# Two chained causal attentions: turning the maxima and packing the values by transfers instead of on TensorE

## The chip, the cores and the metric

The kernel runs on one core of a Trainium2 chip. TensorE multiplies matrices, VectorE, ScalarE and GpSimd (POOL in the profile) do the rest, and SyncE (SP) issues transfers. The metric is the device time of one execution in microseconds, the median of several runs. Everything is float32; many operands of TensorE are marked float32r.

## The reference, cut to what matters

There are 32 sequences of 512 tokens and 256 channels. Each is one block: two chained attentions, a layer norm, experts, a second layer norm. The experts act on the first sequence only, since their tokens are 512.

```python
q, k = x @ W_attn + b_attn          # 16 heads of 16 channels
v = x                               # by heads
y  = causal_attn(q, k, v)
e  = v[1:] - y[:-1]
k2 = x[:-1] @ W_k2 + b_k2
y2 = causal_attn(q[1:], k2, e)      # a row of zeros is put ahead of it
x = layernorm(x + y @ W_proj + b_proj + y2 @ W_proj + b_proj)
x = layernorm(x + experts(x))
```

The second attention takes its values from the results of the first, one token on.

## The kernel before, in words

A *group* is four heads of one sequence; there are 4 groups a sequence and 128 in all. The program is a software pipeline of *steps*, one for each group (`step`, L654). A step has five *slots* and a *gap* after each (`rest[0]` to `rest[4]`). The order of TensorE's and SP's instructions is the program's own (L67); the queues of VectorE, ScalarE and GpSimd are ordered by a scheduler when the program is built. Every queue is worked off in its order.

A slot (L393) interleaves two streams of small products on quarters of TensorE's array:
- `maxima` (L271), tiles `sm`: queries by keys for both attentions (a = 0 and 1), with a bfloat16 product that hides what is not causal. VectorE takes the largest score of each query (L325, tile `top`). The tiles `sm` take two pairs of banks of PSUM in turn, one for each pair of heads. So a slot can only begin its first product once VectorE has read the pair of the slot before.
- `scores` (L353), tiles `sc`: the same products transposed, keys by queries, of a group one or two steps older. The negated maximum is added by a third product (`k == 2`, L363), whose moving operand is `m`. ScalarE takes the exponential (L382), GpSimd hides the diagonal block (L386).

In the gaps:
- `project` (L219, tiles `pj`) makes queries and keys of a pair of groups (`two`); ScalarE adds the bias (`pk`), GpSimd splits it into two float32r parts (`lead`, `pk`), and `spread` (L243) copies these by SP's transfers into the interleaved layout `q_t` and `kk_t`.
- `halve` and `augment` (L329, L334) split a group's maxima into two parts, turn them on TensorE (four transposes, tile `mt`) and copy them to `m` by ScalarE. `m` is used from slot 2 of the next step.
- `values` (L426, tiles `av`) multiplies the exponentials with the values, for the first attention in gap 1 and for the second in gap 4 (two steps after the maxima). The 17th column of each head is 1, so it gives the sum of the exponentials. ScalarE copies the result (`avs`).
- `normalize` (L444) turns `avs` back by four transposes (tile `yt`) and divides by the sums. For the first attention the result gives `e_pad`, the values of the second (GpSimd, L474); it stands in gap 2. For the second it is added to `y` (L478), in gap 3 of the next step.
- `turn` (L509, eight transposes a sequence, tile `ys`) turns `y` for the output projection, `attended` (L518, tiles `po`), which comes two to four steps later, with a layer norm on VectorE and GpSimd.

SP issues all transfers of the loop: eight a step for `spread`, plus each sequence's loads and its store.

Of the kernel before, what the change touches and what calls it, by code (L numbers as in the profile page):

```python
# [17 lines left out]
P = 128  # L18
# [3 lines left out]
NH2 = 2  # L22
EPS = 1e-5
PER = 4
HV = HD + 1
# [14 lines left out]
def block_kernel(  # L40
# [32 lines left out]
    psum = ctx.enter_context(tc.tile_pool(name="psum", bufs=1, space=bass.MemoryType.PSUM))  # L73

# [101 lines left out]

    v_pad = const.tile([P, NB, NG * GH * HV + HS - HV], F32, name="v_pad")
    e_pad = const.tile([P, NB, NG * GH * HV + HS - HV], F32, name="e_pad")
# [3 lines left out]
    mx = [const.tile([P, NB, GH, HS], F32, name=f"mx{i}") for i in range(2)]  # L182
    for t in mx:
        nc.vector.memset(t, 0.0)
# [3 lines left out]
    def by_head(t):  # L188
        return t[:, :, 0 : NG * GH * HV].rearrange("p n (h s) -> p n h s", s=HV)


    groups = {}
    moving = {}

# [15 lines left out]
    def prepare(n):  # L210
        b, g = divmod(n, NG)
        s = seqs[b]
        heads = slice(g * GH, (g + 1) * GH)
        nc.gpsimd.tensor_copy(
            by_head(v_pad)[:, :, heads, 0:HD], s["x"].rearrange("p n (h d) -> p n h d", d=HD)[:, :, heads]
        )
# [26 lines left out]
    def spread(two, m, which=range(2)):  # L243

        for k in which:
            n = 2 * two + k
            d = groups.setdefault(n, {})
            d["q"] = q_t[n % len(q_t)]
            d["kk"] = kk_t[n % len(kk_t)]
            rows = slice(k * GH * HD, (k + 1) * GH * HD)  # L250
            for i, t in enumerate(moving[two, m]):
                if m == 0:
                    for r in range(2):
                        nc.sync.dma_start(d["q"][r::2, i], t[rows])
                else:
                    nc.sync.dma_start(d["kk"][i::2, m - 1], t[rows])
        if 1 in which:
            del moving[two, m]

    units = [
        ([(2, 0, 1, 0), (0, 0, 1, 3)], 2, 1, (0, 2)),
        ([(3, 0, 1, 0)], 3, 1, (0, 1)),
        ([(1, 0, 2, 0)], 1, 2, (1, 3)),
        ([(2, 1, 1, 0), (0, 1, 1, 3)], 2, 1, (2, 4)),
        ([(3, 1, 1, 0)], 3, 1, (2, 3)),
    ]

    def maxima(n, u, pair):  # L271
# [44 lines left out]
        for i, a, na, at in parts:  # L316
            to = d["top"][:, i, NH2 * pair : NH2 * (pair + 1), a : a + na]
            if alone:
                views += [(part(ps[hh], i, na, at), to[:, hh : hh + 1]) for hh in range(NH2)]
            else:  # L320
                views.append((part(ps[0], i, na, at), to))
# [7 lines left out]
    def halve(n):  # L329
        t, top = mx[n % 2], groups[n]["top"]  # L330
        nc.vector.tensor_copy(half(t[:, :, :, 0:2]), top)
        nc.vector.tensor_sub(half(t[:, :, :, 2:4]), top, t[:, :, :, 0:2])

    def augment(n):  # L334
        d = groups[n]
        ps = bank(f"mt{n}")
        for i in range(NB):
            nc.tensor.transpose(ps[:, i * P : (i + 1) * P], mx[n % 2][:, i].rearrange("p h s -> p (h s)"), ident)  # L338
        d["m"] = grp.tile([P, T], F32, tag="m", name=f"m{n}")
        nc.scalar.copy(half(d["m"]), ps)  # L340

    banks = [
        [(1, 0, 0)],
        [(1, 1, 0), (1, 3, 3)],
        [(0, 2, 0), (1, 2, 2)],
        [(0, 0, 0)],
        [(0, 1, 0), (0, 3, 3)],  # L350
    ]

    def scores(n, u, pair):  # L353
        parts = [p for p in banks[u] if 0 <= n - p[0] < n_all]
# [7 lines left out]
        def score(d, a, j, at, k, hh, rows):  # L362
            keys = minus[a][rows] if k == 2 else d["kk"][rows, a, j * P : (j + 1) * P]  # L363
            queries = d["m"][rows] if k == 2 else d["q"][rows, k]
            nc.tensor.matmul(  # L365
                ps[hh][:, at * P : at * P + T - j * P],
                half(keys),
                half(queries[:, j * P :]),
                start=(k == 0),
                stop=(k == 2),  # L370
            )

        for a, j, at in parts:
            groups[n - a]["pt", a, j, pair] = pt[:, :, at * P : at * P + T - j * P]
            for k in range(3):
                todo.append((T - j * P, partial(score, groups[n - a], a, j, at, k)))

        def exponentials():
# [5 lines left out]
            for a, j, at in parts:  # L384
# [41 lines left out]
    def values(n, a):  # L426
# [3 lines left out]
        ps = bank(f"av{n}_{a}")  # L430
        order = [0, 2, 1, 3] if a == 0 else [0, 1, 3, 2]
        for j in order:
            for h in range(GH):
                nc.tensor.matmul(  # L434
                    ps[HS * h : HS * (h + 1), j * P :],
                    vals[:, j, (g * GH + h) * HV : (g * GH + h) * HV + HS],
                    d["pt", a, j, h // NH2][:, h % NH2],
# [3 lines left out]
        avs = d["avs", a] = work.tile([P, T], F32, tag="avs", name=f"avs{n}_{a}")  # L441
        nc.scalar.copy(avs, ps)  # L442

    def normalize(n, a):  # L444
        b, g = divmod(n, NG)
        d, s = groups[n], seqs[b]
        ps = bank(f"yt{n}_{a}")
        for i in range(NB):
            nc.tensor.transpose(ps[:, i * P : (i + 1) * P], d["avs", a][:, i * P : (i + 1) * P], ident)  # L449
        got = ps.rearrange("p (n h s) -> p n h s", h=GH, s=HS)  # L450
        if a:

            kept = work.tile([P, NB, GH, HV], F32, tag="kept", name=f"kept{n}", bufs=2)
            nc.scalar.copy(kept, got[:, :, :, 0:HV])
            got = kept
        rden = small.tile([P, NB, GH], F32, tag="rden", name=f"rden{n}_{a}")
        sums = got[:, :, :, HD]
        if a:

            den = small.tile([P, NB, GH], F32, tag="den", name=f"den{n}")  # L460
            nc.vector.tensor_scalar_max(den, sums, 1e-30)
            sums = den
        nc.vector.reciprocal(rden, sums)
        rb = rden.unsqueeze(3).to_broadcast([P, NB, GH, HD])
        cols = slice(g * GH * HD, (g + 1) * GH * HD)

        def heads(t):
            return t[:, :, cols].rearrange("p n (h d) -> p n h d", d=HD)

        if a == 0:  # L470
            if g == 0:
                s["y"] = seq.tile([P, NB, C], F32, tag="y", name=f"y{b}")
            nc.vector.tensor_mul(heads(s["y"]), got[:, :, :, 0:HD], rb)
            nc.gpsimd.tensor_sub(by_head(e_pad)[:, :, g * GH : (g + 1) * GH, 0:HD], heads(s["xs"]), heads(s["y"]))  # L474
        else:
            y2 = work.tile([P, NB, GH * HD], F32, tag="y2", name=f"y2_{n}", bufs=1)
            nc.vector.tensor_mul(y2.rearrange("p n (h d) -> p n h d", d=HD), got[:, :, :, 0:HD], rb)
            nc.gpsimd.tensor_add(s["y"][:, :, cols], s["y"][:, :, cols], y2)  # L478
            groups.pop(n)
# [28 lines left out]

    def turn(b):  # L509
        s = seqs[b]  # L510
        ysT = s["ysT"] = work.tile([P, NC, T], F32, tag="ysT", name=f"ysT{b}", bufs=1)
        for c in range(NC):
            ps = bank(f"ys{b}_{c}")
            for i in range(NB):
                nc.tensor.transpose(ps[:, i * P : (i + 1) * P], s["y"][:, i, c * P : (c + 1) * P], ident)  # L515
            nc.scalar.copy(ysT[:, c], ps)
# [137 lines left out]
    def step(n):  # L654
# [3 lines left out]
        if r == 1 and b + 1 < B:  # L658
            load(b + 1)
        if r == 3 and b + 1 < B:  # L660
# [157 lines left out]
```

## Time and profile before

| what | us |
|---|---|
| median of three runs | 2645.53 (2642.57 to 2645.70) |
| the profiled execution | 2650.03 |
| its span, first to last instruction | 2648.3 |
| TensorE busy | 2569.7 |
| VectorE busy | 1943.7 |
| ScalarE busy | 1757.0 |
| GpSimd busy | 1724.0 |
| share of the 16 DMA engines that SP's transfers took | 33.1% |

The span is that of one execution; sums over its rows are made against 2650.03 and then moved by the 4.5 us that lie between it and the median. A group's "mean" in the profile is the length of one instruction, and many of TensorE's overlap, so the pieces of the chain of waits say better what a product costs in time. In lines of the trace the columns are start, length, engine, line, operation, output from input, count; in brackets stands the idle time before it and what ended it. Lines of windows give, for each engine, busy time and number of instructions, then TensorE's granted clock as a share, the DMA share and GB/s.

### The profile page before, as it was taken

The numbers are of one execution on the slowest core, as the hardware profiler recorded it, in microseconds if no ns is written. First come the engines' busy times: TensorE is split into PE (matmuls) and PEld (weight loads), VectorE is DVE, ScalarE is ACT, GpSimd is POOL, SyncE is SP. The second block draws the span as 40 slices with busy tenths as digits, with TensorE's granted clock in tenths as the row PEclk, the third lists the DMA queues.
The fourth block names the chain that finished last, engine by engine and source line by source line (L and its number), as shares of the span: only waits on it lengthen the run. The fifth ranks groups of instructions, "written<-read, shape, count | busy, mean of one in ns | idle before, by whom it ended". The sixth has DMA issues, their size and how long they took to land.

```text
span 2648.3 us, 82677 instructions
## 1 busy us (share of the span) xinstructions
PE 2569.7 (97%) x33808; PEld 1742.7 (66%) x33808; DVE 1943.7 (73%) x3225; ACT 1757.0 (66%) x3416; POOL 1724.0 (65%) x3318
## 2 busy tenths in 40 slices
PE   6999999999999999999999999999999999999997
PEld 3666666666666666666666666666666666666665
DVE  5777777677777777777777777777777777777773
ACT  2666554467777767776767777676777767677774
POOL 4555555567666676766667666666766666676664
PEclk7999999999999999999999999999999999999998
DMA  5233233233334343333433333343333334233320
GB/s 136 69 89 89 73 85 91 79 81 97 89 75 104 83 104 82 95 90 74 105 81 99 88 91 93 75 105 81 90 96 90 94 76 104 82 90 96 88 67 25
DMA packets 167402, 231.91 MB, mean 88 GB/s; under 512 B 21624, under 2 KB 91248, under 8 KB 167024
## 3 DMA queue, kind: packets, MB, share of 16 engines
q1 hardware_dynamic: 164592, 226.17, 33.1%
q8 instruction: 269, 4.41, 0.7%
q14 instruction: 109, 0.89, 0.1%
q10 hardware_dynamic: 2368, 0.42, 0.1%
q0 software_dynamic: 64, 0.02, 0.0%
HBM read 75.41 MB, written 16.78 MB: 35 GB/s over the span
## 4 chain that ended last, share of the span: by engine, by line
PE 91%; ACT 3%; issue 2%; POOL 2%; DVE 2%; DMA 1%; SPq 0%; ACTq 0%; POOLq 0%; DVEq 0%
PE sc L365 28%; PE av L434 22%; PE pj L223 13%; PE sm L301 10%; PE yt L449 6%; PE po L526 4%; PE mt L338 3%; ACT pt L382 2%; PE gu L607 2%; PE ys L515 1%; PE dn L630 1%; DVE top L325 1%; PE sm L286 1%; POOL pk L241 0%; DMA bp_qk<-in_b_qkk 0%
## 5 line engine op out<-in xcount | busy, mean ns | idle before, releaser
L325 DVE TENSOR_REDUCE top<-sm 128x2 f32<-128x768 f32 (+3 forms) x1800 | 1536.3, 907 | 589.0 <-PE sc L365 328.7
L382 ACT ACTIVATE pt<-sc 128x512 f32<-128x512 f32 (+1 forms) x2564 | 1323.3, 602 | 322.9 <-PE sc L365 315.9
L386 POOL TENSOR_SCALAR_AFFINE_SELECT pt<-pt 128x256 f32<-128x256 f32 x2048 | 787.7, 407 | 531.1 <-ACT pt L382 530.3
L301 PE MATMUL sm<-kk_t,q_t 32*128 32x512 f32 (+2 forms) x7168 | 1034.8, 381 | 18.7 <-DVE top L325 9.0
L365 PE MATMUL sc<-q_t,kk_t 32*128 32x256 f32 (+3 forms) x8192 | 1045.5, 338 | 3.4 <-DVE h L529 2.0
L365 PEld LDWEIGHTS sc<-q_t,kk_t 32*128 32x128 f32 x8192 | 701.2, 184 | 260.4 <-issue 160.2
L365 PE MATMUL sc<-m,minus 32*128 32x256 f32 (+3 forms) x4096 | 756.4, 318 | 0.0
L301 PEld LDWEIGHTS sm<-kk_t,q_t 32*128 32x128 f32 x7168 | 613.8, 190 | 25.2 <-DVE top L325 11.7
L365 PEld LDWEIGHTS sc<-m,minus 32*128 32x128 f32 x4096 | 507.1, 185 | 10.0
L223 PE MATMUL pj<-xT,wq_sb 128*128 128x256 f32 (+1 forms) x1020 | 400.3, 516 | 8.5 <-DVE wq_sb L112 8.5
L442 ACT COPY avs<-av 128x512 f32<-128x512 f32 x256 | 150.2, 587 | 325.9 <-PE av L434 325.9
L286 PE MATMUL sm<-hide,pick 32*128 32x256 bf16 (+1 forms) x2560 | 339.2, 258 | 0.0
L434 PE MATMUL av<-pt,e_pad 128*32 128x512 f32 (+3 forms) x4096 | 304.2, 437 | 17.9 <-ACT pt L382 13.3
L434 PE MATMUL av<-pt,v_pad 128*32 128x512 f32 (+3 forms) x4096 | 304.4, 437 | 14.6 <-POOL pt L386 4.2
L235 ACT ACTIVATE pk<-pj,bp_qk 128x256 f32<-128x256 f32 (+1 forms) x255 | 151.2, 593 | 194.7 <-PE pj L223 185.4
L241 POOL TENSOR_TENSOR pk<-pk,lead 128x512 fp32r<-128x512 f32 x192 | 244.7, 1274 | 15.7 <-ACT lead L240 5.0
L434 PEld LDWEIGHTS av<-pt,v_pad 128*32 128x32 f32 x4096 | 136.8, 110 | 170.3 <-issue 128.4
L223 PEld LDWEIGHTS pj<-xT,wq_sb 128*128 128x128 f32 x1020 | 176.1, 192 | 96.1 <-issue 65.1
L434 PEld LDWEIGHTS av<-pt,e_pad 128*32 128x32 f32 x4096 | 130.9, 110 | 152.8 <-issue 148.0
L478 POOL TENSOR_TENSOR y<-y,y 128x256 f32<-128x256 f32 x128 | 96.4, 753 | 118.7 <-DVE mv L542 68.2
L449 PE MATMUL yt<-ident,avs 128*128 128x128 f32 x1024 | 168.0, 287 | 2.1 <-ACT pt L382 0.9
L449 PEld LDWEIGHTS yt<-ident,avs 128*128 128x128 f32 x1024 | 109.2, 141 | 75.3 <-ACT pt L382 70.3
(90 smaller groups left out, 1980.5 us busy)
## 6 DMA issues: line engine op xcount, KB each, us to landing
q_t<-lead SPq DMA_DIRECT2D x256, 128.0 KB
q_t<-pk SPq DMA_DIRECT2D x256, 128.0 KB
kk_t<-lead SPq DMA_DIRECT2D x256, 128.0 KB
kk_t<-pk SPq DMA_DIRECT2D x256, 128.0 KB
xT<-in_xT SPq DMA_DIRECT2D x32, 512.0 KB
x<-in_x SPq DMA_DIRECT2D x32, 512.0 KB
xr<-in_x SPq DMA_DIRECT2D x32, 512.0 KB
out<-h SPq DMA_DIRECT2D x31, 512.0 KB
```

Of the source, the lines that this page charges most:

```text
L223: nc.tensor.matmul(ps[:, 0 : hi - lo], wq_sb[:, m, c, part * P : (part + 1) * P], seqs[b]["xT"][:, c, lo:hi], start=(c == 0), stop=(c == N ...
L235: nc.scalar.activation(pk[:, lo:hi], ps[:, 0 : hi - lo], AF.Identity, bias=bp_qk[:, m, part : part + 1])
L241: nc.gpsimd.tensor_sub(half(pk), pk, lead)
L286: nc.tensor.matmul(ps[hh][:, 0 if alone else hh].rearrange("p (k c) -> p k c", c=P)[:, first::step], pick[rows], hide[rows, kinds[0] : kin ...
L301: nc.tensor.matmul(part(ps[hh], i, na, at)[:, 0 if alone else hh], half(d["q"][rows, k, i * P : (i + 1) * P]), half(d["kk"][rows, a : a + ...
L325: nc.vector.tensor_reduce(to, view, AX.X, ALU.max)
L365: nc.tensor.matmul(ps[hh][:, at * P : at * P + T - j * P], half(keys), half(queries[:, j * P :]), start=(k == 0), stop=(k == 2),)
L382: nc.scalar.activation(pt[:, hh, lo:hi], ps[hh][:, lo:hi], AF.Exp, scale=HD**-0.5)
L386: nc.gpsimd.affine_select(diag, diag, pattern=[[0, NH2], [1, P]], compare_op=ALU.is_ge, fill=0.0, base=-a, channel_multiplier=-1,)
L434: nc.tensor.matmul(ps[HS * h : HS * (h + 1), j * P :], vals[:, j, (g * GH + h) * HV : (g * GH + h) * HV + HS], d["pt", a, j, h // NH2][:, ...
L442: nc.scalar.copy(avs, ps)
L449: nc.tensor.transpose(ps[:, i * P : (i + 1) * P], d["avs", a][:, i * P : (i + 1) * P], ident)
```

## The change

- **Maxima.** VectorE transposes the split maxima in blocks of 32 by 32 (`tr`). One transfer writes them to DRAM, four read them into `m` (`m_t`, two fixed tiles), which now lies in runs of 32 queries. The four transposes on TensorE and ScalarE's copy go.
- **Values.** The two groups of a pair use one padded tile with interleaved columns, so that a strided transfer can pick the values out of `avs` (`num`) and another the sums (`sums`, to DRAM). `inverse` reads all sums of a pair of groups, for both attentions, into one tile `den` of 128 by 64 and inverts it; `unload` writes the inverses to DRAM (`inv`); `widen` reads them back, each row onto 16 partitions (`r`, 2 loads of 256 KB); `weigh` multiplies both `num` by `r` and adds them to `ysT`. The second attention's `yt`, the copy `kept`, the tile `y` and `turn` go.
- **Gaps.** Slots are rotated by one: what was slot 4 comes first. The scores of the first attention's second and fourth block of keys come a step later. All projections are made in halves. The second attention's values are made in two parts, in gaps 3 and 4. The output projection comes one piece a step. `inverse`, `unload`, `widen` and `weigh` stand in gaps 0 to 3 of even steps.

```diff
+    dram = ctx.enter_context(tc.tile_pool(name="dram", bufs=2, space=bass.MemoryType.DRAM))
...
     units = [
+        ([(3, 0, 1, 0)], 3, 1, (0, 1)),
         ([(2, 0, 1, 0), (0, 0, 1, 3)], 2, 1, (0, 2)),
-        ([(3, 0, 1, 0)], 3, 1, (0, 1)),
+        ([(3, 1, 1, 0)], 3, 1, (2, 3)),
         ([(1, 0, 2, 0)], 1, 2, (1, 3)),
         ([(2, 1, 1, 0), (0, 1, 1, 3)], 2, 1, (2, 4)),
-        ([(3, 1, 1, 0)], 3, 1, (2, 3)),
     ]
...
     def halve(n):
-        t, top = mx[n % 2], groups[n]["top"]
+        d = groups[n]
+        top = d.pop("top")
+        t = small.tile([P, NB, GH, 4], F32, tag="mx", name=f"mx{n}", bufs=2)
         nc.vector.tensor_copy(half(t[:, :, :, 0:2]), top)
         nc.vector.tensor_sub(half(t[:, :, :, 2:4]), top, t[:, :, :, 0:2])
+        tr = small.tile([P, RUN], F32, tag="tr", name=f"tr{n}", bufs=2)
+        nc.vector.transpose(tr, t.rearrange("p n h s -> p (n h s)"))
+        d["rows"] = dram.tile([P, RUN], F32, tag="turned", name=f"turned{n}")
+        nc.sync.dma_start(d["rows"], tr)
 
     def augment(n):
         d = groups[n]
-        ps = bank(f"mt{n}")
-        for i in range(NB):
-            nc.tensor.transpose(ps[:, i * P : (i + 1) * P], mx[n % 2][:, i].rearrange("p h s -> p (h s)"), ident)
-        d["m"] = grp.tile([P, T], F32, tag="m", name=f"m{n}")
-        nc.scalar.copy(half(d["m"]), ps)
+        m = d["m"] = m_t[n % 2]
+        rows = d.pop("rows").rearrange("(r k h s) c -> s h (r k) c", k=2, h=GH, s=4)
+        for s in range(4):
+            nc.sync.dma_start(m[s::HS].rearrange("h (r c) -> h r c", c=RUN), rows[s])
 
     banks = [
-        [(1, 0, 0)],
-        [(1, 1, 0), (1, 3, 3)],
-        [(0, 2, 0), (1, 2, 2)],
-        [(0, 0, 0)],
-        [(0, 1, 0), (0, 3, 3)],
+        [(0, 1, 0, 1), (0, 3, 3, 1)],
+        [(1, 0, 0, 1)],
+        [(1, 1, 0, 1), (1, 3, 3, 1)],
+        [(0, 2, 0, 0), (1, 2, 2, 1)],
+        [(0, 0, 0, 0)],
     ]
...
-    def values(n, a):
+    def values(n, a, lo=0, hi=T):
...
+    def gather(n, a):
+        two, k = divmod(n, 2)
+        p = packed.setdefault(two, {})
+        if k == 0:
+            p[a] = work.tile([P, T], F32, tag=f"num{a}", name=f"num{two}_{a}", bufs=2 - a)
+        if "sums" not in p:
+            p["sums"] = dram.tile([2, 2, GH, T], F32, tag="sums", name=f"sums{two}")
+        avs = (groups[n] if a == 0 else groups.pop(n))["avs", a]
+        nc.sync.dma_start(p["sums"][a, k], avs[(HS - 1) * k :: HS])
+        nc.sync.dma_start(p[a][GH * HD * k : GH * HD * (k + 1)], avs[1 - k :: 2])
+
+    def inverse(two):
+        p = packed[two]
+        t = p["den"] = small.tile([P, RUN], F32, tag="den", name=f"den{two}", bufs=1)
+        nc.sync.dma_start(t, p["sums"].rearrange("a k h (c q) -> (a k h c) q", q=RUN))
+        nc.vector.tensor_scalar_max(t, t, 1e-30)
+        nc.vector.reciprocal(t, t)
+
+    def unload(two):
+        p = packed[two]
+        p["inv"] = dram.tile([2, 2, GH, T], F32, tag="inv", name=f"inv{two}")
+        nc.sync.dma_start(p["inv"].rearrange("a k h (c q) -> (a k h c) q", q=RUN), p["den"])
+
+    def widen(two):
+        p = packed[two]
+        r = p["r"] = work.tile([P, 2, T], F32, tag="r", name=f"r{two}", bufs=1)
+        for a in range(2):
+            nc.sync.dma_start(
+                r[:, a], p["inv"][a].rearrange("k h t -> (k h) t").unsqueeze(1).to_broadcast([2 * GH, HD, T])
+            )
+
+    def weigh(two):
+        b, c = divmod(two, NC)
+        p = packed.pop(two)
+        if c == 0:
+            seqs[b]["ysT"] = work.tile([P, NC, T], F32, tag="ysT", name=f"ysT{b}", bufs=2)
+        for a in range(2):
+            nc.vector.tensor_mul(p[a], p[a], p["r"][:, a])
+        nc.gpsimd.tensor_add(seqs[b]["ysT"][:, c], p[0], p[1])
...
-    def turn(b):
...
+        two, odd = divmod(n, 2)
+        ahead, behind = two + 1, two - 2
...
+        if ready(n - 1):
+            add(0, augment, n - 1)
+        if ready(2 * ahead):
+            if odd:
+                add(0, project, ahead, 0, T // 2)
+                add(0, spread, ahead, 1, 0)
+                add(2, project, ahead, 2, 0, T // 2)
+                add(3, project, ahead, 2, T // 2)
+            else:
+                add(0, project, ahead, 1, 0, T // 2)
+                add(2, project, ahead, 1, T // 2)
+                add(3, project, ahead, 0, 0, T // 2)
+        if ready(2 * behind) and not odd:
+            add(0, inverse, behind)
+        if ready(2 * two) and two and not odd:
+            add(0, spread, two, 0, 1)
+        if ready(n - 2):
+            soon = n > n_all
+            add(0 if soon else 1, values, n - 2, 0)
+            add(0 if soon else 1, gather, n - 2, 0)
+            rest[1 if soon else 2].insert(0, partial(normalize, n - 2))
+            add(3, values, n - 2, 1, 0, T // 2)
+            add(4, values, n - 2, 1, T // 2)
...
+        if ready(2 * behind) and not odd:
+            add(1, unload, behind)
+            add(2, widen, behind)
+            add(3, weigh, behind)
+        if ready(2 * two) and two and not odd:
+            add(1, spread, two, 2, 1)
+        if ready(n):
+            add(4, halve, n)
+        if ready(n - 2):
+            add(4, gather, n - 2, 1)
```

The diff is cut to what the prediction speaks of.

## The prediction

> **What bounds the kernel now.** I read four views, in this order: the page, the chain of waits around 1280 to 1345 us, the timelines of each engine there, and the windows around the few places where TensorE stood still.
>
> From the page: TensorE is busy nearly throughout and carries the chain.
>
> ```profile
> span 2648.3 us, 82677 instructions
> ...
> PE 2569.7 (97%) x33808; PEld 1742.7 (66%) x33808; DVE 1943.7 (73%) x3225; ACT 1757.0 (66%) x3416; POOL 1724.0 (65%) x3318
> ...
> PE 91%; ACT 3%; issue 2%; POOL 2%; DVE 2%; DMA 1%; SPq 0%; ACTq 0%; POOLq 0%; DVEq 0%
> ```
>
> From the chain of waits (start, length, what): transposes, projections and value products stand on the path with nothing beside them.
>
> ```profile
> 1301.58 0.59 PE mt L338 x4
> 1302.16 0.96 PE pj L223 x4
> ...
> 1304.97 2.36 PE av L434 x32
> ...
> 1309.00 0.66 PE yt L449 x4
> 1309.65 1.81 PE pj L223 x4
> ...
> 1313.21 0.59 PE yt L449 x4
> ...
> 1338.04 1.02 PE ys L515 x8
> ```
>
> Between these the five slots of a step last 1.71, 1.84, 1.67, 1.74 and 1.86 us (1299.87 to 1301.58, 1303.13 to 1304.97, and so on). Stores of neighbouring sequences are issued at 1342.23 and 1419.81, so four steps take 77.58 us.
>
> The other engines have slack, but their queues are in order, and a queue that waits stops TensorE. Here VectorE waited 2.37 us inside a layer norm; TensorE stood 4.46 us and then ran at half clock (the column of 0.50 to 1.00):
>
> ```profile
> 524.46 0.69 PE L301 MATMUL sm<-kk_t,q_t 32*128 32x384 f32 x2 [4.46 <-DVE top L325]
> ```
> ```profile
> 520.00:522.00 2.00, 0.00 (x0) 0.00 (x0) 0.35 (x1) 1.08 (x2) 1.83 (x5) 1.00 0.00 0
> 522.00:524.00 2.00, 0.00 (x0) 0.00 (x0) 2.00 (x5) 0.00 (x0) 0.80 (x2) 0.63 0.00 0
> 524.00:526.00 2.00, 1.54 (x16) 1.07 (x16) 1.93 (x5) 0.00 (x0) 0.00 (x0) 0.50 0.91 256
> 526.00:528.00 2.00, 2.00 (x9) 1.78 (x8) 1.34 (x3) 1.63 (x3) 0.41 (x1) 0.50 0.98 298
> 528.00:530.00 2.00, 2.00 (x27) 1.35 (x27) 0.07 (x1) 0.47 (x1) 0.00 (x0) 0.66 0.69 241
> ```
>
> A wait of 1.58 us for a DMA did the same: the clock was 0.50 from about 62 to 68.7 us.
>
> ```profile
> 59.99 0.52 PE L301 MATMUL sm<-kk_t,q_t 32*128 32x384 f32 x8 [1.58 <-DMA q_t<-pk]
> ```
>
> **What is removed from the path**, per two steps (two groups of heads). The maxima's transposes: 2 x 0.59 = 1.18 us. The second attention's `yt`: 0.59 + 0.66 = 1.25. The eight `ys` transposes, 1.02 per sequence: 0.51. Together 2.94.
>
> **What is added to the path.** The two whole projections become halves: 2 x 0.96 for 1.81, so 2 x 0.11 = 0.22. The second attention's value product is split (384 and 896 of 1280 columns) into 48 records for 32. The trace has no split one: its bounds are 0 and 0.37 per split, one opening `sc` piece after a switch; I take 0.2, near the middle, so 0.4 per two steps. TensorE's net is 2.94 - 0.22 - 0.4 = **2.3 us saved per two steps**, and 64 x 2.3 = 147 us in all. The product with `m` now reads runs of 32 elements. Nothing shows such runs; the nearest row is a `sm` product over two runs of 256, which takes 0.49 us like one over a single run of 512, so I take 0 (upper bound: 4096 x 0.318 us doubled, four abreast, 326 us).
>
> **Beside the path.** ScalarE loses 128 x (0.417 + 0.617) + 64 x 0.59 = 170 us and gains some 70 in half-size copies. VectorE loses 128 x (0.167 + 0.248 + 0.562) = 125 and gains 128 products at 0.67 (as L583's 128x512) and some 60 in small operations. GpSimd loses 128 x 0.753 and gains 64 x 1.28. All of it is hidden by TensorE. SP's queue gets 1408 DMAs more on 1279; at 0.55 us an issue (L256's median is 0.546 to 0.587) it is some 1480 us busy, 56%. Bytes go from 232 to about 314 MB, the DMA share from 33% to about 45%.
>
> **The new waits.** I lay one even step of the changed kernel out from zero, with po in its first gap. The rotated slots are 1.86, 1.71, 1.84, 1.67, 1.74:
> - slot 0, projection, po: 3.78; slot 1: 5.49; first values (2.36): 7.85
> - slot 2: 9.69; `yt`, projection: 11.31; slot 3: 12.98
> - projection 13.94; first half of the second values (0.7 by columns): slot 4 starts at 14.65
>
> *The maxima.* They are turned about 0.3 us into the next step. Write, then four reads: the nearest landings are 2.1 and 2.4 us (the 8 and 16 KB loads `b_dn` and `b_gu`). Issue 0.4, landed 2.5, reads issued to 4.7, landed 7.1 (9 at the 4.3 of a 512 KB load). They are due in slot 3, about 11.7: hidden. Were that cover gone, each us late would cost 128 us, as every step has it.
>
> *The inverted sums.* Behind the gather of the last step come `sums`, `num`, the four reads, then `den`: issued at about 5, landed at 7.3. VectorE has `den` queued before slot 1's reductions, which could start at 4.8 (1.0 after their slot, as 1300.89 stands to 1299.87). Slot 2 wants their banks at 7.85, less 1.2 for the first reduction and 0.5 for `den`'s two operations: `den` should land by about 6.2 and is 1.1 us late.
>
> *The widened inverses.* SP has, in this order, the first values' `sums` and `num`, then the write of `inv`, then the read of `r`. The values' copy ends 0.64 us after the product (1307.33 to 1307.97), at 8.5. Two issues later `inv` goes out at 9.6 and lands at 11.7. `r` is two loads, 512 KB. Nearest row: `xr`, also 512 KB, issued at 1334.50; GpSimd began on it at 1338.82, after waiting:
>
> ```profile
> 1334.50 0.38 SPq L501 DMA_DIRECT2D xr<-in_x  x1
> ```
> ```profile
> 1338.82 1.29 POOL L507 TENSOR_TENSOR xr<-xr,bp 128x512 f32<-128x512 f32 x1 [0.49 <-DMA xr<-in_x]
> ```
>
> So 4.3 us, and `r` is there at 16.0. In all 62 full even steps VectorE's queue as built has both products with `r` *before* slot 3's reductions; in about half the first also stands before `y`, which e_pad and the first half of the second values need. Products 2 x 0.67: 17.35; first reduction 1.2: 18.55. Slot 4 wanted these banks at 14.65: **TensorE is stopped 3.9 us** per even step. The 1.1 us of `den` is inside, since it only moves TensorE towards the same moment. Bounds: `r` as fast as a small load (2.1): 1.7 us. With a 512 KB store ahead of it, as in every other even step: `r` at 18.5, 6.4 us. I take 3.9, from the row of equal size.
>
> *The clock.* After such a stop the rows above show 5.0 us (524.46 to 529.5) to 6.7 us at half clock: 2.5 to 3.4 us lost; I take 3.0.
>
> [...]
>
> [...]
>
> **The sum.** Per even step -2.3 + 3.9 + 3.0 = +4.6; x 62 = +285. Experts' steps (five even ones) carry `down` and one more hidden product between the first values and slot 4, some 2 us of cover: -10. At the end, `values` to `po` took 4.5 us (2628.76 to 2633.27); now 2.1 + 2.6 + 0.5 + 2.1 + 4.3 + 1.3 + 1.3 = 14: +9. The profiled execution took 2650.0 us (span 2648.3), so 2650 + 284 = 2934; the runs' median is 4.5 lower: **2930 us**. With the bounds: per even step -2.3 + 1.7 + 2.5 = 1.9 gives 2763; -2.3 + 6.4 + 3.4 = 7.5 gives 3110.
>
> **The rivals.**
> 1. *The cover holds, faster.* If `r` lands by 12.1 (14.65 less 1.2 and 1.34), TensorE loses nothing but `den`'s 0 to 1.1 us: 2645 - 147 + 9 = 2507, to 2575. For it: TensorE's 97%, and DMAs of which few were ever waited for. Against it: from 8.5 to 12.1 there are 3.6 us for three issues and two round trips.
> 2. *Stop without clock.* 2645 + 62 x 1.6 = 2745, or down to 2610 at the lower bound of the stop. [...] Against it: the 1.58 us row.
> 3. *Worse:* `m` late as well, or half clock spreading, above 3110. Against it: a slower TensorE hides more of the DMAs.
>
> **Chances.** Forecast 0.52 (2763 to 3110), rival 1 0.18, rival 2 0.24 (a fifth of it at or below the old time), rival 3 0.06. A measurement of this kernel tells about 0.2% from no change. Faster 0.20, same 0.03, slower 0.77. Leaving rivals 1 and 3 out would drop 0.24, so the range reaches down over rival 1: 2505 to 3110; the forecast's own range is 2763 to 3110.
>
> **What would show it.** Right: TensorE idle before slot 4's `sm` in even steps, released by VectorE's reductions; VectorE idle before the `num` product, released by DMA `r`; clock cells under 1.0 all along; `mt` and `ys` gone and step pairs near 43 us. Wrong: VectorE's products starting without idle time, clock 1.0, and step pairs near 36.5.

## The result and the profile after

The changed kernel takes **3221.24 us** (median, 3216.51 to 3232.12); the kernel before took 2644.05 in the same session. The ratio is 1.219 (95% interval 1.216 to 1.222): slower by 577 us, where 285 were forecast, and above the range.

The page of the changed kernel:

```profile
span 3216.7 us, 87313 instructions
...
PE 2660.5 (83%) x35080; PEld 1872.1 (58%) x35080; DVE 2015.1 (63%) x3227; ACT 1677.0 (52%) x3350; POOL 1723.4 (54%) x3254
...
PEclk8998999889899989888988889998889888989997
```

TensorE is idle for 3216.7 - 2660.5 = 556.2 us, where it was 2648.3 - 2569.7 = 78.6. It is also busy for 90.8 us more, with less to do: the mean granted clock fell from 0.989 to 0.892. 477.6 + 90.8 is the whole difference of the spans, 568.4. What TensorE waited for (engine, tile and line, releaser, us in total, times, longest):

```profile
PE sm L300 <- DVE top L324: 176.7, 85, 5.5
PE av L440 <- POOL e_pad L506: 171.1, 30, 7.1
PE sc L371 <- DVE y L504: 88.0, 32, 5.9
```

The first and third lines are the stop that was forecast: slot 4 waits for VectorE's reductions, or for `y`, and VectorE waits for `den` and `r`. In one even step, in VectorE's timeline (start, length, then the idle time ahead of it in brackets):

```profile
1626.41 0.33 DVE L467 TENSOR_SCALAR den<-den 128x64 f32<-128x64 f32 x1 [1.98 <-DMA den<-sums]
...
1636.55 0.69 DVE L489 TENSOR_TENSOR num<-num,r 128x512 f32<-128x512 f32 x1 [4.00 <-DMA r<-inv]
1638.02 0.69 DVE L489 TENSOR_TENSOR num<-num,r 128x512 f32<-128x512 f32 x1 [0.78 <-DMA r<-inv]
```

TensorE's first product of slot 4 then:

```profile
1639.90 0.69 PE L300 MATMUL sm<-kk_t,q_t 32*128 32x384 f32 x2 [3.86 <-DVE top L324]
```

TensorE's windows at the same place (busy times of the engines, then granted clock, DMA share and GB/s) show the stop and the half clock behind it, until the clock is back at 1.00:

```profile
1636.00:1638.00 2.00, 0.04 (x2) 0.00 (x0) 0.69 (x1) 0.10 (x1) 0.00 (x0) 1.00 0.34 127
1638.00:1640.00 2.00, 0.10 (x4) 0.10 (x4) 1.98 (x3) 0.00 (x0) 1.21 (x1) 0.61 0.00 0
1640.00:1642.00 2.00, 2.00 (x26) 1.88 (x30) 1.57 (x2) 0.78 (x2) 1.50 (x5) 0.50 0.00 0
...
1646.00:1648.00 2.00, 1.87 (x39) 1.62 (x34) 1.51 (x2) 1.32 (x4) 0.06 (x1) 1.00 0.09 27
```

The second line of the waits, 171.1 us in 30 places, has no place in the prediction. It comes once in a sequence, from GpSimd. GpSimd's timeline in one of these steps:

```profile
1609.41 2.48 POOL L534 TENSOR_TENSOR xr<-xr,bp 128x512 f32<-128x512 f32 x2 [5.03 <-DMA xs<-in_x]
1611.84 0.77 POOL L387 TENSOR_SCALAR_AFFINE_SELECT pt<-pt 128x256 f32<-128x256 f32 x2
1612.57 0.73 POOL L506 TENSOR_TENSOR e_pad<-xs,y 128x256 f32<-128x256 f32 x1
```

GpSimd stands 5.03 us and begins with the two bias additions to the residual `xr`, whose load SP had issued at 1604.50. The releaser is named `xs` here, but `xs` was issued after it, from 1607.68, and the additions read `xr`. In the sum over all steps it is `xr`, with 144.5 us, where the kernel before had 21.3 (27 times):

```profile
1604.50 0.54 SPq L528 DMA_DIRECT2D xr<-in_x  x1
```
```profile
POOL xr L534 <- DMA xr<-in_x: 144.5, 29, 6.3
```

Behind the additions in the queue stand affine selects and `e_pad`'s subtraction, and TensorE's next product (`av` of the second attention) starts at 1613.36 after 5.83 us. The cause lies in lines of the diff that neither the front part nor the prediction speaks of:

```diff
-            if n == (end + 2 if last else end + 3):
-                rest[3].append(lambda b=b: load_residual(b))
+            if n == (end + 2 if last else end + 4):
+                add(1, load_residual, b)
+            if n == (end + 3 if last else end + 4):
+                add(3, biased, b, 0)
+                add(4, biased, b, 1)
```

`end` is the last group's step of sequence `b`. The load moved from the step before the additions into the step of the additions, and the scheduler put both additions ahead of slot 2's `e_pad`.

### The profile page after: what moved, and what is told of

Read it like the earlier page. It is cut to its first block, busy times and chain, and to the rows that moved or that the text cites. A ratio compares the mean times of both kernels' runs of the same rounds, so it can differ in the third digit from the quotient of the medians.

```text
span 3216.7 us, 87313 instructions
## 1 busy us (share of the span) xinstructions
PE 2660.5 (83%) x35080; PEld 1872.1 (58%) x35080; DVE 2015.1 (63%) x3227; ACT 1677.0 (52%) x3350; POOL 1723.4 (54%) x3254
## 3 DMA queue, kind: packets, MB, share of 16 engines
q1 hardware_dynamic: 259824, 308.01, 35.4%
## 5 line engine op out<-in xcount | busy, mean ns | idle before, releaser
L324 DVE TENSOR_REDUCE top<-sm 128x2 f32<-128x1024 f32 (+4 forms) x1802 | 1533.2, 905 | 566.6 <-PE sc L371 362.0
L300 PE MATMUL sm<-kk_t,q_t 32*128 32x512 f32 (+2 forms) x7168 | 1125.9, 409 | 187.5 <-DVE top L324 176.7
L371 PE MATMUL sc<-m_t,minus 32*128 32x256 f32 (+3 forms) x4096 | 727.0, 335 | 0.0
L440 PE MATMUL av<-pt,e_pad 128*32 128x256 f32 (+1 forms) x6144 | 400.6, 403 | 177.7 <-POOL e_pad L506 171.1
L371 PEld LDWEIGHTS sc<-m_t,minus 32*128 32x128 f32 x4096 | 451.8, 198 | 12.3
L449 ACT COPY avs<-av 128x256 f32<-128x256 f32 (+1 forms) x384 | 170.7, 444 | 518.2 <-issue 363.7
L227 PEld LDWEIGHTS pj<-xT,wq_sb 128*128 128x128 f32 x1524 | 286.3, 208 | 119.7 <-ACT pt L383 58.1
L489 DVE TENSOR_TENSOR num<-num,r 128x512 f32<-128x512 f32 x128 | 96.7, 755 | 291.9 <-DMA r<-inv 271.2
L534 POOL TENSOR_TENSOR xr<-xr,bp 128x512 f32<-128x512 f32 x64 | 79.4, 1262 | 157.2 <-DMA xr<-in_x 144.5
L490 POOL TENSOR_TENSOR ysT<-num,num 128x512 f32<-128x512 f32 x64 | 81.0, 1265 | 148.4 <-DVE num L489 148.4
## 6 DMA issues: line engine op xcount, KB each, us to landing
q_t<-lead SPq DMA_DIRECT2D x256, 128.0 KB
q_t<-pk SPq DMA_DIRECT2D x256, 128.0 KB
kk_t<-lead SPq DMA_DIRECT2D x256, 128.0 KB
kk_t<-pk SPq DMA_DIRECT2D x256, 128.0 KB
num<-avs SPq DMA_DIRECT2D x256, 128.0 KB
```

Source lines behind the costliest of these rows:

```text
L227: nc.tensor.matmul(ps[:, 0 : hi - lo], wq_sb[:, m, c, part * P : (part + 1) * P], seqs[b]["xT"][:, c, lo:hi], start=(c == 0), stop=(c == N ...
L300: nc.tensor.matmul(part(ps[hh], i, na, at)[:, 0 if alone else hh], half(d["q"][rows, k, i * P : (i + 1) * P]), half(d["kk"][rows, a : a + ...
L324: nc.vector.tensor_reduce(to, view, AX.X, ALU.max)
L371: nc.tensor.matmul(to, half(keys), half(queries), start=(k == 0), stop=(k == 2))
L440: nc.tensor.matmul(ps[HS * h : HS * (h + 1), first - lo : hi - lo], vals[:, j, first_of(g, h) : first_of(g, h) + HS], d["pt", a, j, h // N ...
L449: nc.scalar.copy(d["avs", a][:, lo:hi], ps[:, 0 : hi - lo])
```

## The experiments

Theory A: the time went to instructions that wait for a transfer in an engine's in-order queue, with what TensorE needs behind them, and to the half clock after each such stop. The rivals: the wait only moves (B); traffic, the strided read of `m` or the split products cost it (C, later D). In the edits `issue_after` queues the block's instructions of an engine behind one named instruction of that engine, with no wait for its end. `red[0]` is the last reduction of `top` traced so far, `sel[0]` the last affine select. "Idle" and "busy" are TensorE's in the profiled execution.

| kernel | median us | ratio to before (95%) | busy | idle | clock |
|---|---|---|---|---|---|
| changed | 3221.2 | 1.219 (1.216 to 1.222) | 2660.5 | 556.2 | 0.892 |
| e1_xr | 3088.4 | 1.168 (1.165 to 1.171) | 2644.2 | 439.2 | 0.912 |
| e4_behind | 3101.5 | 1.172 (1.169 to 1.174) | 2665.4 | 432.0 | 0.907 |
| e6_den | 3122.3 | 1.181 (1.178 to 1.184) | 2636.5 | 479.6 | 0.901 |
| e7_weigh | 2837.6 | 1.073 (1.071 to 1.075) | 2541.9 | 294.2 | 0.942 |
| e2_late | 2762.6 | 1.044 (1.042 to 1.046) | 2473.1 | 290.8 | 0.944 |
| e3_both | 2914.0 | 1.102 (1.099 to 1.105) | 2547.4 | 366.1 | 0.927 |
| e5_late_behind | 2668.6 | 1.009 (1.008 to 1.011) | 2490.5 | 181.4 | 0.968 |
| e9_den2 | 2585.1 | 0.976 (0.975 to 0.978) | 2444.1 | 140.4 | 0.981 |
| e11_den2_xr | 2749.4 | 1.038 (1.036 to 1.039) | 2467.1 | 284.2 | 0.945 |
| e8_mt | 2619.2 | 0.990 (0.988 to 0.993) | 2469.9 | 152.7 | 0.981 |
| e10_den2_mt | 2606.2 | 0.984 (0.983 to 0.986) | 2457.5 | 144.7 | 0.986 |
| e12_aug1 | 2641.1 | 0.998 (0.996 to 0.999) | 2460.8 | 173.6 | 0.975 |
| e13_gap3 | 2576.5 | 0.972 (0.970 to 0.975) | 2432.9 | 146.9 | 0.982 |
| e14_gap3_aug1 | 2654.9 | 1.003 (1.001 to 1.005) | 2465.4 | 182.7 | 0.966 |

### The residual: e1_xr and e4_behind

e1_xr loads it a step earlier:

```diff
-        s["xr"] = seq.tile([P, NB, C], F32, tag="xr", name=f"xr{b}", bufs=1)
+        s["xr"] = seq.tile([P, NB, C], F32, tag="xr", name=f"xr{b}", bufs=2)
...
-            if n == (end + 2 if last else end + 4):
-                add(1, load_residual, b)
+            if n == (end + 2 if last else end + 3):
+                add(3, load_residual, b)
...
-                add(3, biased, b, 0)
-                add(4, biased, b, 1)
+                add(1, biased, b, 0)
+                add(3, biased, b, 1)
```

> One part undone: the residual is loaded a step earlier again (step end+3, gap 3, with a second buffer), and its two bias additions stand in gaps 1 and 3 of step end+4, behind e_pad's subtraction in GpSimd's queue as built. Theory A (stops by queued waits, and half clock after each): the 171.1 us that TensorE waited for e_pad's subtraction go, and some 95 us of half clock with them, so about 3221 - 266 = 2955 us (2900 to 3000), and that is what the recorded sum had for the rest. Theory B (the once-per-sequence stop only covers other lateness, which then shows in the next wait): 3140 us or more. Theory C (the time went to traffic, the strided read of m or the split products, not to stops): within 30 us of 3221.

e4_behind leaves the load late and moves only the additions in GpSimd's queue:

```diff
+        with tc.issue_after(sel[0].ins):
+            nc.gpsimd.tensor_add(t[:, two], t[:, two], bp2.unsqueeze(1).to_broadcast([P, 2, C]))
...
-                add(3, biased, b, 0)
+                add(4, biased, b, 0)
```

> Only the place in GpSimd's queue: the residual is loaded as late as in the changed kernel (step end+4, gap 1), but both bias additions are queued behind the last affine select of slot 4 of that step. Theory A, in the form that the queued wait and not the transfer costs the time: the same as the run with the early load, about 2955 us (2900 to 3010). If the late transfer itself counts (its 512 KB beside num, r and q), less than half of that gain: above 3090 us.

Both kernels lose the wait for `e_pad` (2.3 us are left in each), and they take 133 and 120 us less. So it is the place in the queue that costs nearly all of it, and not the late transfer. (3101 lies above the 3090 that were to speak for the transfer, but that bound was set for a gain of 266 us; of the 133 us that the early load gained, the place alone gives 120.) The price was half of the 266 us expected, and e1_xr lies in the range of no theory. What TensorE no longer waited for GpSimd came back in part as waits for VectorE. VectorE's waits in e4_behind:

```profile
DVE den L468 <- DMA den<-sums: 254.1, 62, 12.1
DVE num L490 <- DMA r<-inv: 224.5, 110, 6.8
```

In the changed kernel `den` was waited for 155.9 us: while TensorE stood for `xr`, SP and the transfers caught up, and the next `den` was early. The trace shows it between 400 and 2400 us: in the even steps right after a load of `xr` the mean wait for `den` is 1.56 us in the changed kernel and 5.14 in e4_behind, in the other even steps 2.92 and 2.87. And TensorE's busy time did not fall (2660.5 and 2665.4), so on balance no clock was won.

### den and r: e2_late, e6_den, e7_weigh

e2_late moves both, and leaves the residual as the change has it:

```diff
     def inverse(two):
...
-        nc.vector.tensor_scalar_max(t, t, 1e-30)
-        nc.vector.reciprocal(t, t)
...
     def unload(two):
         p = packed[two]
+        t = p["den"]
+        with tc.issue_after(red[0].ins):
+            nc.vector.tensor_scalar_max(t, t, 1e-30)
+            nc.vector.reciprocal(t, t)
...
-        for a in range(2):
-            nc.vector.tensor_mul(p[a], p[a], p["r"][:, a])
+        with tc.issue_after(red[0].ins):
+            for a in range(2):
+                nc.vector.tensor_mul(p[a], p[a], p["r"][:, a])
...
-            add(3, weigh, behind)
+            if 2 * behind + 2 == n_all:
+                add(3, weigh, behind)
+        if ready(2 * behind) and odd and 2 * behind + 2 < n_all:
+            add(1, weigh, behind)
```

`num` of the second attention gets a second buffer. 

> One part moved: the two products with r are weighed in gap 1 of the next, odd step, behind slot 1's reductions, and the maximum and reciprocal of den stand behind slot 1's reductions of the even step; all transfers stay (num for the second attention gets a second buffer). The residual is loaded as in the changed kernel. Theory A: TensorE's waits for slot 3's reductions and for y go, about 307 us of the 478 us of added idle time, and the half clock behind them, some 140 us: 3221 - 447 = about 2775 us (2700 to 2860). Theory B (SP's queue or the transfers themselves are what is late, so the wait moves to another place): 3000 us or more. Theory C (traffic, m's strided read or the split products): within 60 us of 3221.

It took 2762.6: 459 us less, as theory A had it. TensorE's waits for `top` and `y` fell to 9.6 and 7.6 us; those for `e_pad` stayed at 167.9.

e6_den and e7_weigh are e4_behind with one half of this edit each.

> From e4_behind (3101 us): only the maximum and reciprocal of den are queued behind slot 1's reductions; the products with r stay in the even step. By the recorded prediction den's lateness lies inside the stop for r, so taking it away gives almost nothing: 3050 to 3101. Theory A as it stands after the first runs (VectorE waits 254 us for den and 225 us for r in e4_behind, one after the other, each with its own stop and half clock): about half of the 580 us between e4_behind and a kernel without stops, so 2780 to 2900.

> From e4_behind (3101 us): only the two products with r are moved, to gap 1 of the next step behind slot 1's reductions; den's maximum and reciprocal stay in front of slot 1's reductions. By the recorded prediction r sets the stop and den's 1.1 us are left: 2520 + 62 x 1.1 (to 62 x 2.6 with clock) = 2590 to 2680. Theory A with two separate stops: den's remains, 2750 to 2850.

Moving `den` alone gained nothing (3122.3, 21 us more). VectorE's wait for `den` fell from 254.1 to 121.2 us and its wait for `r` rose from 224.5 to 367.3, nearly the same sum (478.6 and 488.5). My two separate stops were wrong here: `den`'s lateness lay inside the stop for `r`, as the prediction had said. Moving the products alone gained 264 us, which ends in theory A's range and not in the prediction's 2590 to 2680: `den` now made a stop of its own, and VectorE waited 254.8 us for it. With both moved (e5_late_behind, below) another 169 us went.

### Both together: e3_both, e5_late_behind, e9_den2

e3_both is e1_xr and e2_late together. 

> The edits of the two runs before together. Theory A: no stop is left, TensorE's saving of 147 us shows: 2645 - 147 + some 10 to 60 = 2510 to 2560 us, faster than the kernel before. Theory B: waits that moved keep it at or above 2645. Theory C: within 60 us of 3221.

Theory A failed on it: 2914.0, slower than e2_late alone. It is what theory B had said, a wait that moved. What TensorE waited for in e3_both:

```profile
PE av L441 <- POOL pt L388: 197.5, 34, 8.0
```

The scheduler had put the additions ahead of affine selects of the step before; SP issued the load right behind the two loads of `r`, and GpSimd waited 183.3 us for it. Loading earlier had moved the waiting instruction earlier too. So the additions were placed by hand, as in e4_behind:

> The late weighing and den of run e2_late together with the bias additions queued behind slot 4's last affine select, as in e4_behind (where the early load of e3_both had only moved GpSimd's wait: 183.3 us for xr, and TensorE's 197.1 us for an affine select). Theory A (stops by queued waits): the 168 us that TensorE still stood for e_pad in e2_late go, with some 70 us of clock, so 2763 - 240 = about 2520 us (2500 to 2570), faster than the kernel before. Theory B (transfers themselves late or in each other's way): the wait shows up elsewhere once more and the time stays above 2645.

2668.6 us: 94 us less than e2_late, but no gain on the kernel before, and again above theory B's 2645. VectorE still waited 128.0 us for `den`. SP's timeline in an even step of e5_late_behind shows why:

```profile
1127.95 0.36 SPq L339 DMA_DIRECT2D turned<-tr  x1
...
1132.09 2.27 SPq L347 DMA_DIRECT2D m_t<-turned  x4
1134.46 0.39 SPq L468 DMA_DIRECT2D den<-sums  x1
```

The read of `den` stands behind the four reads of `m`, and these wait on SP for the landing of `turned`: it goes out 6.5 us after `turned` here. VectorE had ended slot 1's reductions at 1133.5 and got `den` at 1136.33. e9_den2 gives it one slot more:

```diff
-            add(1, unload, behind)
-            add(2, widen, behind)
+            add(2, unload, behind)
+            add(3, widen, behind)
```

> From e5_late_behind (2669 us), where VectorE still waited 128 us for den in 48 places, since SP issues den's read behind the four reads of m, which wait for the landing of turned: den's maximum and reciprocal are queued behind slot 2's reductions, a slot later, and the write of inv and the reads of r go one gap later. Theory A (only a queued wait, its cause now SP's order): TensorE's last 80 us of waits for VectorE and their clock go, so 2669 - 100 to 140 = about 2530 to 2570 us, faster than the kernel before. Theory D (the turning of the maxima costs TensorE by itself, by its transfers or its read of m): within 25 us of 2669.

**2585.1 us, 2.4% faster than the kernel before.** Its page, and what TensorE waits for most:

```profile
span 2584.5 us, 87251 instructions
...
PE 2444.1 (95%) x35080; PEld 1743.1 (67%) x35080; DVE 2056.2 (80%) x3227; ACT 1665.2 (64%) x3350; POOL 1719.0 (67%) x3254
```
```profile
PE pj L229 <- DMA xT<-in_xT: 18.3, 16, 2.0
PE av L442 <- ACT pt L385: 15.8, 87, 0.4
PE sm L302 <- DVE top L326: 13.0, 29, 2.3
```

All the computation and all the transfers of the change are still in it; only the places of a few instructions in the queues of VectorE, GpSimd and SP differ, and a second buffer for `num`. So these places cost the 636 us between the two kernels, as theory A says; theories C and D are out for that part. Theory A's number was missed: 84 us were gained where 100 to 140 were expected.

### The residual's stop by itself: e11_den2_xr

e9_den2 with the bias additions back in the changed kernel's place. 

> From e9_den2: the residual's bias additions back to where the scheduler puts them, ahead of slot 2's second pair of affine selects and of e_pad. It is the stop for xr by itself, with no other stop near it. Theory A in the form that a stop lets SP and the transfers catch up and so shortens the next stop: here nothing is left to shorten, so the price is the whole of it, 170 us idle and 60 to 90 us of clock, 230 to 260 us above e9_den2, against the 120 to 133 us that taking it away gave beside the other stops. If its price is what it was there: 120 to 133 us above e9_den2.

164 us more, between the two expectations. Idle rose by 143.8 us (`e_pad` alone stands at 171.9) and busy by 23.0, which is 0.8 us of clock a stop and not 2 to 3. So the price of one stop depends on the others: 120 beside all of them, 94 beside what is left of `den`'s (e2_late to e5_late_behind), 164 with none.

### Turning the maxima: e8_mt and e10_den2_mt

The maxima go back to TensorE and ScalarE, on e5_late_behind and on e9_den2:

```diff
     def augment(n):
-        m = d["m"] = m_t[n % 2]
-        rows = d.pop("rows").rearrange("(r k h s) c -> s h (r k) c", k=2, h=GH, s=4)
-        for s in range(4):
-            nc.sync.dma_start(m[s::HS].rearrange("h (r c) -> h r c", c=RUN), rows[s])
+        ps = bank(f"mt{n}")
+        for i in range(NB):
+            nc.tensor.transpose(ps[:, i * P : (i + 1) * P], mx[n % 2][:, i].rearrange("p h s -> p (h s)"), ident)
+        d["m"] = grp.tile([P, T], F32, tag="m", name=f"m{n}")
+        nc.scalar.copy(half(d["m"]), ps)
```

> From e5_late_behind: the maxima are turned by TensorE and copied by ScalarE again, as in the kernel before; no transfers of turned and m_t, and the product with m reads one run. It tells what the first part of the change is worth when nothing stops. By the recorded prediction (2 x 0.59 us saved per two steps, m hidden, the read of m in runs of 32 free): 64 x 1.18 = 75 us slower than e5_late_behind, about 2595 us. If the runs of 32 cost TensorE time or m is late: within 25 us of e5_late_behind, or faster.

> From e9_den2: the maxima turned by TensorE and ScalarE again, no transfers of turned and m_t. Theory A: 75 us slower than e9_den2 (64 x 1.18 us), about 2620 us, near e8_mt's 2619 where den was hardly waited for. Theory D: faster than e9_den2.

On e5_late_behind this was 49 us *faster*: with no wait for `turned` on SP, the read of `den` goes out sooner, and VectorE's wait for it is 38.2 us instead of 128.0. The time is that of the second expectation, the reason is another. On e9_den2, where `den` has time, it was 21 us slower, not 75. The read of `m` in runs of 32 costs nothing to speak of: the product with `m` has a mean of 319 ns in e9_den2 and of 317 with whole runs.

### Where e9_den2 lacks 83 us: e12_aug1, e13_gap3, e14_gap3_aug1

The sum without the stops is 2645.5 - 142.6 - 10 + 9 = 2502. e12_aug1 moves `augment` from the first place of gap 0 to the first of gap 1, so that SP does not stand for `turned`.

> From e9_den2 (2585 us): the four reads of m are issued in gap 1 ahead of the first values, behind den's read and the q and kk spreads of gap 0, no longer first in gap 0, where SP stood 280 us for the landing of turned with the rest of the step's transfers behind it. e9_den2 is some 80 us above the sum's 2507 and only 21 us under the kernel that turns the maxima on TensorE, where 75 were to be had. If that gap is SP's standing in order (later xT, den, q): 2585 - 25 to 60, so 2525 to 2560 us. If it is the transfers' own traffic or the product's read of m: within 10 us of 2585. If m becomes late instead, as it now lands some 4 us later against a due time of 11.7: slower than 2600.

It was slower, 2641.1: TensorE waited 52.4 us for `m`, in 27 places, and no longer for `xT`. So `m` was covered in the changed kernel, but by less than the delay of this edit.

e13_gap3 and e14_gap3_aug1 move the two additions from behind slot 4's affine selects to behind slot 3's (`add(3, biased, ...)` for both), on e9_den2 and on e12_aug1. In e9_den2 they make VectorE's small operations beside them slow, in VectorE's timeline:

```profile
1397.86 1.27 DVE L334 CAST mx<-top 128x32 fp32r<-128x32 f32 x1
1399.17 1.20 DVE L335 TENSOR_TENSOR mx<-top,mx 128x32 fp32r<-128x32 f32 x1
```

> From e9_den2 (2585 us): the two bias additions move from behind slot 4's affine selects to behind slot 3's. In e9_den2 they run on GpSimd from 1397.82 for 2.50 us, and VectorE's two small operations on mx beside them take 1.27 and 1.20 us where they take 0.18 and 0.19 otherwise, so turned is written 2.1 us later, once per sequence, and with it m and all that SP has queued behind. If that is a part of what e9_den2 lacks of 2502: 30 sequences x 1 to 2 us, so 2525 to 2555 us. If m and SP have that much to spare: within 8 us of 2585.

> From e12_aug1 (2641 us), where TensorE waited 52.4 us for m in 27 places, about once per sequence: the same move of the bias additions. If the slowed operations on mx were what made m late there: the 52.4 us go, 2585 us or less. If m is late for another reason (the xs loads ahead of it on SP): 2620 us or more.

e13_gap3 gained 8.6 us, at the edge of the intervals, far from the 30 to 60 expected, so that is at most a small part. In e14_gap3_aug1 `m` was still late (73.6 us in 29 places), and SP's timeline names the reason:

```profile
1039.90 0.55 SPq L462 DMA_DIRECT2D sums<-avs  x1
...
1044.92 0.36 SPq L468 DMA_DIRECT2D den<-sums  x1
...
1047.86 2.29 SPq L347 DMA_DIRECT2D m_t<-turned  x4
```

SP had issued the loads of `xs` (the next sequence) from 1033.41 on. `sums`, 8 KB, is read back only 5.0 us after its issue, and `m` stands behind that read. In the 25 even steps after loads of `xs` between 400 and 2400 us it was 4.7 us on average, in the other 25 it was 2.0. For TensorE, `m` came mostly 1.5 to 3.9 us late, 2.5 on average. What makes up the rest of the 83 us was not settled: TensorE is idle 140.4 us instead of 78.6, in many kinds of waits, the largest 18.3 us in all, and busy 21 us more than 2569.7 - 147, at a clock of 0.981 instead of 0.989. Over 24 sequences the stores of e9_den2 stand 75.0 us apart, 37.5 for two steps; the sum had 36.5.

## Why the prediction was wrong

The sum against the experiments (medians):

| term | predicted | measured |
|---|---|---|
| the kernel without the stops | 2502 | 2585.1 (e9_den2) |
| stops for `den` and `r`, with clock | 62 x 6.9 = 428 | 516 (e9_den2 to e4_behind) |
| stop for the residual | no term | 120 (e4_behind to changed) |
| sum | 2930 | 3221.2 |

The measured terms are differences along one order of edits, so they add up by construction; in another order each would be different. Of the 291 us above 2930, the residual's stop makes 120, `den` and `r` 88, and what e9_den2 lacks 83.

**The step that failed** is the count of what the change moves, in the sentence on GpSimd: it "loses 128 x 0.753 and gains 64 x 1.28. All of it is hidden by TensorE." Only busy time was counted. The load of the residual was moved into the step of its bias additions, so two instructions in GpSimd's queue got a wait of up to 6.3 us, ahead of `e_pad`. The rule was applied to VectorE's queue and not to GpSimd's, though the row quoted for `xr`'s price, issued at 1334.50 and used at 1338.82, was that very transfer. GpSimd's wait for `xr` went from 21.3 to 144.5 us. The stop is worth 120 us here and 164 alone.

**The stop for `r`** was right as a mechanism. VectorE waited 4.00 us in the step above, then 0.78, and TensorE stood 3.86 us before slot 4, where 3.9 were forecast. From e5_late_behind to e4_behind, with `den` and the products both back in front, TensorE's idle time rises by 250.6 us and its busy time by 174.9, per even step 4.04 and 2.82, where 3.9 and 3.0 stood in the sum. But the agreement is in part luck, since two errors go against each other. The 4.3 us for `r` were too short. SP issued both loads here:

```profile
1632.94 1.33 SPq L479 DMA_DIRECT2D r<-inv  x2
```

VectorE started on the first at 1636.55, 3.6 us later, and on the second, for which it waited again, at 1638.02, after 5.1 us. Over 41 even steps between 400 and 2400 us the second started 5.9 us after the issue on average, 5.5 where no store stands ahead and 6.2 where one does, as here. Counted from the step's begin (0.4 us ahead of `turned` at 1619.82), the second product started at 18.6, and `r` was to be there at 16.0, or at 18.5 behind a store. But TensorE also came to slot 4 at 16.6 instead of 14.65; 0.83 us of that is a wait for VectorE in slot 2, behind `den`.

The DMA share (the number before the last) was 0.50, at 189 GB/s, while these two loads ran, and 0.95, at 238 GB/s, from 1609.60, while other loads did:

```profile
1635.20:1635.60 0.40, 0.40 (x14) 0.19 (x6) 0.00 (x0) 0.27 (x1) 0.08 (x1) 1.00 0.50 189
1609.60:1610.00 0.40, 0.00 (x0) 0.00 (x0) 0.00 (x0) 0.00 (x0) 0.40 (x1) 1.00 0.95 238
```

Why the loads of `r` ran at that share was not shown. The 4.3 of the sum came from `xr`, a load of the same size in the kernel before; the 5.9 above is what `r` took.

**`den`** was under-sized. Its lateness was put at 1.1 us, with its read issued 4.7 us after `turned`. In the changed kernel the issue comes 4.69 us after it (mean of 41 even steps), and VectorE waits 155.9 / 59 = 2.6 us. In e4_behind, where no stop for `xr` gives SP time, the issue comes 5.9 us after it on average and up to 7.9, and the wait is 254.1 / 62 = 4.1. "Inside the stop for `r`" held (e6_den), but with `r` moved away `den` cost 169 us at one place in the queue, and 84 more went between e5_late_behind and e9_den2, which make the second term 516.

**What TensorE saves** was over-sized: 2.3 us for two steps; e9_den2 shows 38.7 - 37.5 = 1.2 (the kernel before: 77.4 us between stores on the mean of 22 sequences). In busy time the miss is small, 125.6 us less where 147 were forecast; the rest is idle time, 61.8 us more than before. The turned maxima were to be worth 75 us and are worth 21.

**`m` hidden** and the free read in runs of 32 held.

**The rivals.** 1 (the cover holds) and 2 (no clock) did not happen: TensorE's busy time in the changed kernel is 216 us above that of e9_den2, with the same products. Rival 3, above 3110, came true in the time, but not by its mechanism: `m` was not late, and the half clock cost these 216 us where 62 x 3.0 = 186 stood in the sum. The step pairs, 43 us forecast, were 48.0 (18 sequences, 96.06 us each). The DMA share was put at 45% and was 35.4%, since the same bytes took a longer time.

## What to carry to other kernels

List every instruction that the change gives a wait for a transfer, on every engine, GpSimd's additions included, and read in the built queue what stands behind it; busy time tells nothing of that. A result that goes by way of DRAM wants its consumer some slots later, behind the work that others wait for: here three such moves of two to three slots, with the computation unchanged, took 3221 us to 2585. The prices of stops don't add up (the residual's was 94, 120 or 164 us), since a stop gave the transfers time that shortened the next one (1.56 us for `den` instead of 5.14 in the even steps after a load of `xr`); measure each with the others gone as well.

## What the runs showed of the hardware

- **Half clock came in multiples of 3.41 us.** Read from windows of 0.4 us it lasted from 1611.14 to 1617.97 and from 1638.45 to 1645.27 in the changed kernel (6.8), from 1436.4 to 1439.8 in e4_behind (3.4) and from 1302.65 to 1312.9 in e11_den2_xr (10.2). The changed kernel's trace has 113 stretches of half clock; 112 are 1, 2, 3, 5 or 8 times 3.41 us long, and the last, of 6.77 us, ends with the trace. All 113 begin at whole multiples of 3.4133 us counted from the first, to within 0.001 us; the two starts above are 27.31 us apart, eight times 3.41. The first of these two began 3.6 us after TensorE's last product, that in e11_den2_xr 2.0 us after it; in e4_behind half clock followed 2.02 us of idle time, and in the kernel before the 1.58 us of the prediction's row at 59.99. How little idle time is enough was not measured, nor what sets the spacing.
- **The residual's stop cost little clock when alone.** In e11_den2_xr TensorE's busy time rose by 0.8 us a stop, where the stops for `den` and `r` cost 2.8. A part of the half clock lies inside the stop (3.9 us of the 10.2 above), but that is not the whole reason: by the granted clocks (0.945 of 2751.3 us, 0.981 of 2584.5, and only 1.0 and 0.5 in the clock records of the changed kernel) half clock lasted some 303 us, against 98 in e9_den2. This estimate is 6.8 us more for each of 30 stops, and some 4 us if the same share as above lies inside the stop. The rest of the reason stays open.
- **VectorE was slower beside GpSimd's additions.** The operation of 0.18 us on `mx` took 1.27 in e9_den2 while GpSimd ran its two additions of 512 columns (1397.82, 2.50 us together). On the mean of 128 it took 0.448 us there and 0.317 in e13_gap3, with the additions moved. Why it was slower was not shown.
- **A small transfer landed later behind large ones**: `sums`, 8 KB, was read back 5.0 us after its issue behind the loads of `xs`, and 2.0 on average where no such loads stand ahead of it (e14_gap3_aug1); `turned`, 32 KB, was read back 2.3 us after its issue in the step at 1619.82 of the changed kernel.
